# Two ways to carry attention values to the output: merged weights on averaged inputs, or token-wise values averaged head by head

## The chip, the cores and the metric

The kernel runs on one core of a Trainium2 chip. The metric is device time in microseconds (us), the median of several executions; lower is better. The profile is one execution taken with the hardware profiler. Its engines are TensorE (PE, with the weight loads as a row of their own, PEld), VectorE (DVE), ScalarE (ACT), GpSimd (POOL), and the queues that issue transfers (SP, and ACT's and POOL's own).

## What is computed

The input is 2048 tokens of 128 features. It goes through a transformer of six layers, a selective state-space block, and the same transformer once more, with residual sums around them. The change touches the transformer alone. One layer of it, cut to what matters here:

```python
x = normalised input
qkv = shift_tokens(x) @ Wqkv            # 16 heads of 64 features each for q, k and v
q, k = rotary(l2norm(q) * qs), rotary(l2norm(k) * ks)
# windows of 32 tokens: each looks at its own window and at the one before it
attn = softmax(mask(q . k * 8))         # 32 x 64 per head and window
x = x + concat_heads(attn @ v) @ Wo     # Wo: 1024 x 128
a, gate = split(layernorm(shift_tokens(x)) @ W1 + b1)
x = x + (a * gelu(gate)) @ W2 + b2
```

## The kernel before, in words

Activations are kept with the 128 features on the partitions and the 2048 tokens along the free axis (`r0` before attention, `r1` after it). A layer is cut into 16 tiles of 128 tokens (four windows), and the feed-forward part works on blocks of 512 tokens, four tiles each. Everything is float32, and TensorE runs each float32 matmul as two records (x2 in its counts), except transposes, which are one.

`run` goes through 96 + 7 iterations, and in each of them through the list `ORDER`. An entry `("PX", 4)` means: the step PX for the tile whose number is 4 less than that of the iteration. Steps of different tiles thus stand beside each other, and the order in the list is the order in which each of PE, DVE, ACT and POOL runs its own instructions (`manual_schedule`); SP is not in that set. Feed-forward steps (F1, XC, SF, V, VE, XN, G, GL, A, H, Y, YR) run only for every fourth tile.

The steps of one tile, with lines of the profile:

- PQ, PK (`project`, L263): queries and keys, two matmuls each, 128x128 weights against 512 columns, into a double PSUM bank.
- SQ, SK (L275), UQ, UK (L302): squares on ACT and their sums per head on DVE. NL (`roots`, L311 to L316): ACT clips the sums, takes a logarithm and an exponential for a first inverse root, and squares it. NN (`norms`, L320 and L322): one Newton step in two small DVE instructions. T1, T2 (L281, L287), A (L296), C (L326): the rotary products on DVE, their sum and the scaling by the norm on POOL.
- RQ, RK (`turn`, L339): eight transposes each; EQ, EK (L348, L353): copies out of PSUM; EP (L360): the last 32 keys of the tile before.
- S (`score`, L376 and L387): the mask, then 64 matmuls of 64x32 weights against 64 columns, packed into eight sub-arrays of TensorE (two halves of the rows by four quarters of the columns).
- ES, MX, SB, EX, SM, DV: softmax with ACT, DVE and POOL; TP (`flip`, L435): DVE transposes the probabilities in 32x32 squares.
- XT, EXW (`inputs`, `inputs_out`, L442 to L454): the tile's input is transposed to tokens on the partitions and copied out, and two transfers on ACT's queue (48 KB and 16 KB) make a copy that is shifted by one window.
- PX (`average`, L465): the *inputs*, not the values, are averaged by the probabilities: eight matmuls with 32x128 weights and 512 columns (16 heads by 32 queries), four of them side by side in the four quarters of the rows. EZ0, EZ1 (L477): two copies of 128x1024 out of PSUM.
- ZM (`mix`, L485): 16 matmuls, one per head, with 128x128 weights against 128 columns, add up over the heads. The weights are `m`, the product of a head's value weights and output weights. `merge` (L207, L214) makes them once per layer in the first pass and stores them in memory; the second pass loads them.
- RS (L495): residual sum on DVE.
- VE (`variance_out`, L534 to L537) makes the feed-forward norm's variance and first inverse root on ACT; XN (`normal`, L544 to L548) is its Newton step and product, five instructions of 128x512 on POOL.

PSUM has a ring of three double banks (tag `w`: x_ps, t_ps, s_ps, z_ps, two thirds of g_ps and a_ps) and one of two single banks (tag `n`: i_ps, y_ps, c_ps, v_ps, o_ps and the rest). A step that takes a bank waits until the readers of the tile that had it are done.

Of the kernel before, what the change touches and what calls it, by code (L numbers as in the profile page):

```python
# [61 lines left out]
    ("SB", 3), ("GL", 7), ("PK", 0), ("AQ", 1), ("T1K", 0), ("SK", 0), ("ZM", 5), ("UQ", 1),  # L62
    ("RS", 5), ("T2K", 0), ("A", 7), ("EX", 3), ("XN", 6), ("RK", 2), ("H", 7), ("RQ", 2),
    ("EK", 2), ("SM", 3), ("UK", 0), ("EQ", 2), ("NL", 1), ("F1", 5), ("XT", 3), ("NN", 1),
    ("PX", 4), ("PQ", 0), ("AK", 0), ("EP", 2), ("DV", 3), ("EZ0", 4), ("CQ", 1), ("CK", 1),
    ("XC", 5), ("S", 2), ("EXW", 3), ("SF", 5), ("EZ1", 4), ("T2Q", 0), ("V", 5), ("ES", 2),
    ("TB", 3), ("T1Q", 0), ("G", 6), ("Y", 7), ("SQ", 0), ("MX", 2), ("VE", 5), ("TP", 3),
    ("YR", 7),
# [76 lines left out]
class Transformer:  # L145
# [7 lines left out]
    def __init__(self, k, x, again, sb, wp, ps):  # L153
        self.k, self.nc, self.x, self.again = k, k.nc, x, again
        self.sb, self.wp, self.ps = sb, wp, ps
        self.at = [Ctx() for _ in range(DEPTH * NT)]
        for st in self.at:
            st.x, st.rot, st.sq, st.t2 = {}, {}, {}, {}
        self.ff = [Ctx() for _ in range(DEPTH * NB)]
        self.w = [Ctx() for _ in range(DEPTH)]  # L160
        self.tabs = {}
        self.r0 = wp.tile([P, PAD + N + 1], F32, tag="r0", name="r0", bufs=1)
        self.r1 = wp.tile([P, PAD + N + 1], F32, tag="r1", name="r1", bufs=1)
# [9 lines left out]
    def load(self, layer):  # L173
        nc, k, wp, w = self.nc, self.k, self.wp, self.w[layer]
        w.qk = wp.tile([P, 2 * INNER], F32, tag="qk", name="qk")
        nc.sync.dma_start(out=w.qk, in_=k.d_wqk[layer])
        if self.again:
            w.m = wp.tile([P, 8, 2, P], F32, tag="m", name="m")
            nc.sync.dma_start(out=w.m.rearrange("p c j f -> p (c j f)"), in_=k.merged[layer])
            return  # L180
        w.v = wp.tile([P, 8, P], F32, tag="wv", name="wv", bufs=1)
        nc.sync.dma_start(out=w.v, in_=k.d_wv[layer].rearrange("(c p) f -> p c f", p=P))
        w.o = wp.tile([P, 8, P], F32, tag="wo", name="wo", bufs=1)
# [11 lines left out]

    def merge(self, layer):

        nc, w = self.nc, self.w[layer]
        if self.again:
            return  # L200
        w.m = self.wp.tile([P, 8, 2, P], F32, tag="m", name="m")
        for half in range(2):
            m_ps = self.bank2("m_ps").rearrange("p j (c f) -> p j c f", f=P)
            for c in range(4):
                for par in range(2):
                    rows = slice(64 * par, 64 * par + 64)
                    nc.tensor.matmul(  # L207
                        out=m_ps[:, par, c, :],
                        lhsT=w.v[rows, 4 * half + c, :],
                        rhs=w.o[rows, 4 * half + c, :],  # L210
                        start=True,
                        stop=True,
                    )
            nc.scalar.copy(  # L214
                w.m[:, 4 * half : 4 * half + 4].rearrange("p c j f -> p j c f"), m_ps
            )
        nc.sync.dma_start(
            out=self.k.merged[layer], in_=w.m.rearrange("p c j f -> p (c j f)")
        )

    def biases(self, layer):
# [19 lines left out]
        nc.scalar.activation(w.w1, w.w1, AF.Identity, scale=self.vec(V_G + layer))  # L241
# [17 lines left out]
    def project(self, g, kind):  # L259
        nc, st = self.nc, self.at[g]  # L260
        x = self.bank2("x_ps")
        for j in range(2):
# [3 lines left out]
                rhs=self.w[g // NT].qk[:, bass.ds(kind * INNER + j * 512, 512)],  # L266
# [3 lines left out]
        st.x[kind] = x.rearrange("p j (h d) -> p (j h) d", d=DH)  # L270
# [36 lines left out]


    def roots(self, g):
        nc, k, st = self.nc, self.k, self.at[g]  # L310
        nc.scalar.activation(st.ss, st.ss, AF.Relu, bias=k.minus_tiny)  # L311
        st.y = self.sb.tile([P, 2, HEADS], F32, tag="y0", name="y0")
        nc.scalar.activation(st.y, st.ss, AF.Ln, bias=k.tiny)
# [4 lines left out]
    def norms(self, g):  # L318
        nc, st = self.nc, self.at[g]
        nc.vector.scalar_tensor_tensor(st.y2, st.ss, 1e-24, st.y2, ALU.add, ALU.mult)  # L320
        st.rn = self.sb.tile([P, 2, HEADS], F32, tag="rn", name="rn")
        nc.vector.scalar_tensor_tensor(st.rn, st.y2, 1.5, st.y, ALU.subtract, ALU.mult)  # L322
# [116 lines left out]
    def inputs(self, g):  # L439
        st = self.at[g]  # L440
        st.i_ps = self.bank("i_ps")[:, 0:P]
        self.nc.tensor.transpose(  # L442
            st.i_ps, self.r0[:, bass.ds(PAD + g % NT * P, P)], self.k.ident
        )

    def inputs_out(self, g):


        nc, st = self.nc, self.at[g]
        st.xw = self.sb.tile([P, 2, P], F32, tag="xw", name="xw", bufs=3)  # L450
        nc.scalar.copy(st.xw[:, 1], st.i_ps)
        nc.scalar.dma_start(out=st.xw[WIN:, 0], in_=st.xw[0 : P - WIN, 1])
        if g % NT:
            nc.scalar.dma_start(out=st.xw[0:WIN, 0], in_=self.at[g - 1].xw[P - WIN :, 1])  # L454
        else:
            nc.gpsimd.memset(st.xw[0:WIN, 0], 0.0)

    def average(self, g):

        st = self.at[g]  # L460
        st.z = [self.bank2("z_ps"), self.bank2("z_ps")]
        for j in range(2):
            for b in range(4):
                rows = slice(32 * b, 32 * b + 32)
                self.nc.tensor.matmul(  # L465
                    out=st.z[b // 2][:, b % 2].rearrange("p (h q) -> p h q", q=WIN),
                    lhsT=st.xw[rows, j, :],
                    rhs=st.pt[rows, :, j, :],
                    start=(j == 0),
                    stop=(j == 1),  # L470
                )

    def averages_out(self, g, half):
        st = self.at[g]
        if half == 0:
            st.zt = self.sb.tile([P, 4, HEADS, WIN], F32, tag="zt", name="zt")
        self.nc.scalar.copy(  # L477
            st.zt[:, 2 * half : 2 * half + 2].rearrange("p b h q -> p b (h q)"), st.z[half]
        )

    def mix(self, g):
        st = self.at[g]
        st.y_ps = self.bank("y_ps")[:, 0:P]
        for h in range(HEADS):
            self.nc.tensor.matmul(  # L485
                out=st.y_ps.rearrange("p (b q) -> p b q", q=WIN),
                lhsT=self.w[g // NT].m[:, h // 2, h % 2, :],
                rhs=st.zt[:, :, h, :],
                start=(h == 0),
                stop=(h == HEADS - 1),  # L490
# [40 lines left out]
    def variance_out(self, f):  # L531
        nc, k, sb, ff = self.nc, self.k, self.sb, self.ff[f]
        ff.ve = sb.tile([P, 512], F32, tag="ve2", name="ve", bufs=1)
        nc.scalar.activation(ff.ve, ff.v_ps, AF.Identity, bias=k.eps, scale=1.0 / P)  # L534
        ff.rs = sb.tile([P, 512], F32, tag="fsq", name="rs", bufs=1)
        nc.scalar.activation(ff.rs, ff.ve, AF.Ln)
        nc.scalar.activation(ff.rs, ff.rs, AF.Exp, scale=-0.5)  # L537

    def normal(self, f):


        nc, ff = self.nc, self.ff[f]
        ff.xn = t = self.sb.tile([P, 512], F32, tag="xn", name="xn", bufs=1)
        nc.gpsimd.tensor_tensor(t, ff.rs, ff.rs, ALU.mult)  # L544
        nc.gpsimd.tensor_tensor(t, t, ff.ve, ALU.mult)
        nc.gpsimd.tensor_scalar(t, t, -0.5, 1.5, ALU.mult, ALU.add)
        nc.gpsimd.tensor_tensor(t, t, ff.rs, ALU.mult)
        nc.gpsimd.tensor_tensor(t, ff.xc, t, ALU.mult)  # L548
# [523 lines left out]
```

## Time and profile before

| what | us |
|---|---|
| median of 3 runs (lowest, highest) | 3694.47 (3687.63, 3701.53) |
| the profiled execution | 3694.83 |
| its span, first to last instruction | 3693.0 |
| first pass: first q/k projection, last matmul of the last layer (L263, L600) | 43.3, 1608.7 |
| second pass: the same | 2105.8, 3681.0 |

Between the passes lies the state-space block. 1.8 us of the profiled execution lie outside its span.

A row of the table of groups gives line, engine, operation, what is written and read with shapes, and the count; then busy time in us and the mean of one in ns; then the idle time of the engine just before such instructions and what ended it. Busy times of PE overlap and their ends are modelled: how long a step holds TensorE is read from the start of its first matmul to the start of the next step's first, in the timeline. In a table of stretches, each engine's busy time is followed by the count of its instructions in brackets.

### The profile page before, as it was taken

The numbers are of one execution on the slowest core, as the hardware profiler recorded it, in microseconds if no ns is written. First come the engines' busy times: TensorE is split into PE (matmuls) and PEld (weight loads), VectorE is DVE, ScalarE is ACT, GpSimd is POOL, SyncE is SP. The second block draws the span as 40 slices with busy tenths as digits, with TensorE's granted clock in tenths as the row PEclk, the third lists the DMA queues.
The fourth block names the chain that finished last, engine by engine and source line by source line (L and its number), as shares of the span: only waits on it lengthen the run. The fifth ranks groups of instructions, "written<-read, shape, count | busy, mean of one in ns | idle before, by whom it ended". The sixth has DMA issues, their size and how long they took to land.

```text
span 3693.0 us, 93340 instructions
## 1 busy us (share of the span) xinstructions
PE 3483.3 (94%) x41200; PEld 2167.3 (59%) x41200; DVE 3020.2 (82%) x3477; ACT 2338.7 (63%) x3414; POOL 2784.8 (75%) x1606
## 2 busy tenths in 40 slices
PE   6999999999999999976999879999999999999997
PEld 3666666666666666632222345666666666666664
DVE  4988888888888888737988767888888888888883
ACT  3767676767767676734222267767676767676764
POOL 5989989898889898720100188999899998998983
PEclk8999999999999999986877889999999999999998
DMA  3010010100100000000000100010100000000000
GB/s 110 12 52 12 23 46 17 40 23 23 35 29 17 29 12 12 6 7 0 0 0 0 68 10 17 22 34 12 35 23 29 23 22 24 28 18 11 17 6 15
DMA packets 64893, 85.12 MB, mean 23 GB/s; under 512 B 8364, under 2 KB 53352, under 8 KB 61416
## 3 DMA queue, kind: packets, MB, share of 16 engines
q1 hardware_dynamic: 34344, 66.74, 5.4%
q10 hardware_dynamic: 30144, 12.41, 1.5%
q8 instruction: 324, 5.31, 0.6%
q14 instruction: 81, 0.66, 0.1%
HBM read 59.39 MB, written 7.34 MB: 18 GB/s over the span
## 4 chain that ended last, share of the span: by engine, by line
PE 78%; DVE 10%; issue 5%; ACT 4%; POOL 2%; ACTq 1%; DMA 0%; POOLq 0%; SPq 0%; DVEq 0%
PE x_ps L263 18%; PE y_ps L485 17%; PE z_ps L465 10%; PE s_ps L387 7%; PE t_ps L339 4%; PE g_ps L556 4%; PE a_ps L556 3%; PE o_ps L600 3%; DVE t L287 3%; PE y L863 3%; DVE st L856 2%; PE s_ps L376 2%; PE c_ps L845 1%; DVE r L495 1%; PE b_ps L845 1%
## 5 line engine op out<-in xcount | busy, mean ns | idle before, releaser
L296 POOL TENSOR_TENSOR rot<-rot,t 128x1024 f32<-128x1024 f32 x384 | 907.3, 2368 | 209.7 <-DVE t L287 207.6
L485 PEld LDWEIGHTS y_ps<-zt,m 128*128 128x128 f32 x6144 | 720.5, 193 | 99.0 <-issue 88.5
L263 PE MATMUL x_ps<-qk,r 128*128 128x512 f32 x1536 | 758.6, 617 | 10.3 <-ACT sq L275 5.1
L326 POOL TENSOR_TENSOR rot<-rot,rn 128x1024 f32<-128x1024 f32 x384 | 722.4, 1902 | 49.6 <-DVE rn L322 49.4
L485 PE MATMUL y_ps<-zt,m 128*128 128x128 f32 x6144 | 722.8, 276 | 5.9 <-ACT zt L477 5.5
L275 ACT ACTIVATE sq<-x_ps 128x1024 f32<-128x1024 f32 x384 | 394.7, 1028 | 378.8 <-DVE rot L281 378.0
L287 DVE TENSOR_TENSOR t<-x_ps,tab 128x1024 f32<-128x1024 f32 x384 | 469.3, 1222 | 82.9 <-PE x_ps L263 73.9
L263 PEld LDWEIGHTS x_ps<-qk,r 128*128 128x128 f32 x1536 | 271.7, 192 | 421.4 <-issue 226.4
L477 ACT COPY zt<-z_ps 128x1024 f32<-128x1024 f32 x384 | 384.9, 1003 | 205.8 <-PE x_ps L263 157.9
L281 DVE TENSOR_TENSOR rot<-x_ps,tab 128x1024 f32<-128x1024 f32 x384 | 464.1, 1209 | 23.4 <-PE x_ps L263 22.0
L302 DVE TENSOR_REDUCE ss<-sq 128x16 f32<-128x1024 f32 x384 | 454.3, 1183 | 0.1
L409 POOL TENSOR_TENSOR pr<-pr,mx 128x1024 f32<-128x1024 f32 x192 | 365.0, 1901 | 76.1 <-DVE mx L403 76.1
L465 PE MATMUL z_ps<-pt,xw 32*128 32x512 f32 x3072 | 400.8, 614 | 13.1 <-DVE t L287 5.2
L339 PE MATMUL t_ps<-cs,rot 128*128 128x128 f32 x3072 | 370.1, 274 | 19.7 <-POOL rot L326 19.7
L425 POOL TENSOR_TENSOR pr<-pr,rs 128x1024 f32<-128x1024 f32 x192 | 365.2, 1902 | 21.3 <-DVE rs L421 13.4
L339 PEld LDWEIGHTS t_ps<-cs,rot 128*128 128x128 f32 x3072 | 345.8, 142 | 50.1 <-issue 25.6
L403 DVE TENSOR_REDUCE mx<-s_ps 128x16 f32<-128x1024 f32 x192 | 235.0, 1224 | 127.1 <-ACT pr L398 125.4
L387 PE MATMUL s_ps<-kt,qt 64*32 64x64 f32 x24576 | 298.5, 227 | 7.0 <-ACT kt L360 7.0
L387 PEld LDWEIGHTS s_ps<-kt,qt 64*32 64x32 f32 x24576 | 267.0, 105 | 55.0 <-issue 45.9
L353 ACT COPY kt<-t_ps 128x1024 f32<-128x1024 f32 x192 | 194.6, 1013 | 146.6 <-PE t_ps L339 143.1
L435 DVE STREAM_TRANSPOSE pt<-pr 128x1024 f32<-128x1024 f32 x192 | 237.4, 1237 | 43.0 <-POOL pr L425 43.0
L850 ACT ACTIVATE da<-delta,a_neg 128x512 f32<-128x512 f32 x128 | 92.2, 722 | 260.3 <-DVE st L856 255.6
(144 smaller groups left out, 4903.2 us busy)
## 6 DMA issues: line engine op xcount, KB each, us to landing
tab<-in_tabs_dram SPq DMA_DIRECT2D x48, 512.0 KB, 3.6
qk<-in_wqk_dram SPq DMA_DIRECT2D x12, 1024.0 KB
m<-m SPq DMA_DIRECT2D x12, 1024.0 KB, 6.4
xw<-xw ACTq DMA_DIRECT2D x192, 48.0 KB, 1.9
w<-in_w_dram SPq DMA_DIRECT2D x12, 341.0 KB, 7.9
wv<-in_wv_dram SPq DMA_DIRECT2D x6, 512.0 KB, 4.3
wo<-in_wo_dram SPq DMA_DIRECT2D x6, 512.0 KB, 8.4
xw<-xw ACTq DMA_DIRECT2D x180, 16.0 KB, 1.9
```

The lines of the kernel that those rows point to most:

```text
L263: nc.tensor.matmul(out=x[:, j], lhsT=self.r0[:, bass.ds(PAD + g % NT * P, P)], rhs=self.w[g // NT].qk[:, bass.ds(kind * INNER + j * 512, 5 ...
L275: self.nc.scalar.activation(st.sq[kind], st.x[kind], AF.Square)
L281: self.nc.vector.tensor_tensor(st.rot[kind], st.x[kind], cos, ALU.mult)
L287: self.nc.vector.tensor_tensor(st.t2[kind].rearrange("p h (two c) -> p h two c", two=2), st.x[kind].rearrange("p h (two c) -> p h two c", ...
L296: self.nc.gpsimd.tensor_tensor(st.rot[kind], st.rot[kind], st.t2[kind], ALU.add)
L302: self.nc.vector.tensor_reduce(st.ss[:, kind, :], st.sq[kind], AX.X, ALU.add)
L326: self.nc.gpsimd.tensor_tensor(st.rot[kind], st.rot[kind], st.rn[:, kind, :].unsqueeze(2).to_broadcast([P, HEADS, DH]), ALU.mult,)
L339: self.nc.tensor.transpose(t_ps[:, c, :], flat[:, bass.ts(c, P)], self.k.ident)
L387: nc.tensor.matmul(out=st.s[32 * b : 32 * b + 32, par, c, :], lhsT=st.qt[rows, c, bass.ts(b, WIN)], rhs=st.kt[rows, c, bass.ds(WIN * b, 2 ...
L465: self.nc.tensor.matmul(out=st.z[b // 2][:, b % 2].rearrange("p (h q) -> p h q", q=WIN), lhsT=st.xw[rows, j, :], rhs=st.pt[rows, :, j, :], ...
L477: self.nc.scalar.copy(st.zt[:, 2 * half : 2 * half + 2].rearrange("p b h q -> p b (h q)"), st.z[half])
L485: self.nc.tensor.matmul(out=st.y_ps.rearrange("p (b q) -> p b q", q=WIN), lhsT=self.w[g // NT].m[:, h // 2, h % 2, :], rhs=st.zt[:, :, h, ...
```

## The change

- Layers load all of Wqkv (`w.qkv`) and Wo (`w.o`). `merge` and the stored product are gone.
- XT and EXW are gone. PV projects the values of a tile (two matmuls as in PQ) into another double bank of the ring, EV copies them out on ACT (128x1024), and VD issues two transfers on SP that make the copy shifted by one window (96 and 32 partitions by 4 KB, that is 384 KB and 128 KB).
- PX works head by head: for each head, window and key window, a matmul with 32x64 weights (values) against 32 columns (probabilities), 128 in all, into eight sub-arrays (four quarters of the rows by two halves of the columns). Its output is half as large, so EZ0 and EZ1 copy 128x512 each.
- ZM uses the output weights: eight matmuls of 128x128 weights against 128 columns.
- NL loses its clipping instruction; a new step FL clips on POOL. NN is three small POOL instructions in place of two on DVE.
- The feed-forward norm stays in PSUM: VE is three ACT instructions, VT does the Newton step in two DVE instructions of 128x512 that read and, the first of them, write `v_ps`. Their result has its sign turned, which `minus_g` in the weights undoes. XN keeps one POOL product.
- `ORDER` is another list, with other lags.

```diff
 ORDER = (
-    ("SB", 3), ("GL", 7), ("PK", 0), ("AQ", 1), ("T1K", 0), ("SK", 0), ("ZM", 5), ("UQ", 1),
-    ("RS", 5), ("T2K", 0), ("A", 7), ("EX", 3), ("XN", 6), ("RK", 2), ("H", 7), ("RQ", 2),
-    ("EK", 2), ("SM", 3), ("UK", 0), ("EQ", 2), ("NL", 1), ("F1", 5), ("XT", 3), ("NN", 1),
-    ("PX", 4), ("PQ", 0), ("AK", 0), ("EP", 2), ("DV", 3), ("EZ0", 4), ("CQ", 1), ("CK", 1),
-    ("XC", 5), ("S", 2), ("EXW", 3), ("SF", 5), ("EZ1", 4), ("T2Q", 0), ("V", 5), ("ES", 2),
-    ("TB", 3), ("T1Q", 0), ("G", 6), ("Y", 7), ("SQ", 0), ("MX", 2), ("VE", 5), ("TP", 3),
-    ("YR", 7),
+    ("VT", 6), ("VD", 3), ("EQ", 2), ("AK", 1), ("UK", 1), ("F1", 5), ("EX", 3), ("S", 2),
+    ("EZ0", 4), ("XC", 5), ("SF", 5), ("EZ1", 4), ("PK", 0), ("UQ", 1), ("FL", 1), ("TB", 7),
+    ("SM", 3), ("V", 5), ("XN", 6), ("ES", 2), ("Y", 7), ("PQ", 0), ("MX", 2), ("NL", 1),
+    ("SK", 0), ("T2K", 0), ("DV", 3), ("G", 6), ("NN", 1), ("CK", 1), ("CQ", 1), ("SB", 2),
+    ("T1K", 0), ("PV", 2), ("SQ", 0), ("YR", 7), ("VE", 5), ("T2Q", 0), ("T1Q", 0), ("A", 6),
+    ("TP", 3), ("GL", 6), ("EV", 2), ("RK", 1), ("H", 6), ("EK", 1), ("AQ", 0), ("ZM", 4),
+    ("EP", 1), ("RQ", 1), ("RS", 4), ("PX", 3),
 )
...
-        if self.again:
-            w.m = wp.tile([P, 8, 2, P], F32, tag="m", name="m")
-            nc.sync.dma_start(out=w.m.rearrange("p c j f -> p (c j f)"), in_=k.merged[layer])
-            return
...
+        w.qkv = wp.tile([P, 3 * INNER], F32, tag="qkv", name="qkv")
+        nc.sync.dma_start(out=w.qkv, in_=k.d_wqkv[layer])
+        w.o = wp.tile([P, 8, P], F32, tag="wo", name="wo")
...
-    def merge(self, layer):
...
-        nc.scalar.activation(w.w1, w.w1, AF.Identity, scale=self.vec(V_G + layer))
+        nc.scalar.activation(w.w1, w.w1, AF.Identity, scale=k.minus_g[:, layer : layer + 1])
...
+        if kind == 2:
+            st.v_ps = x
...
+    def floors(self, g):
+        ss = self.at[g].ss
+        self.nc.gpsimd.tensor_scalar(ss, ss, 1e-24, None, ALU.max)
...
-        nc.scalar.activation(st.ss, st.ss, AF.Relu, bias=k.minus_tiny)
...
-        nc.vector.scalar_tensor_tensor(st.y2, st.ss, 1e-24, st.y2, ALU.add, ALU.mult)
         st.rn = self.sb.tile([P, 2, HEADS], F32, tag="rn", name="rn")
-        nc.vector.scalar_tensor_tensor(st.rn, st.y2, 1.5, st.y, ALU.subtract, ALU.mult)
+        nc.gpsimd.tensor_tensor(st.rn, st.ss, st.y2, ALU.mult)
+        nc.gpsimd.tensor_scalar(st.rn, st.rn, -1.0, 1.5, ALU.mult, ALU.add)
+        nc.gpsimd.tensor_tensor(st.rn, st.rn, st.y, ALU.mult)
...
-    def inputs(self, g):
-    def inputs_out(self, g):
...
+    def values_out(self, g):
         nc, st = self.nc, self.at[g]
+        st.v = self.sb.tile([P, HEADS, DH], F32, tag="v", name="v")
+        nc.scalar.copy(st.v.rearrange("p h d -> p (h d)"), st.v_ps.rearrange("p j f -> p (j f)"))
+
+    def values_before(self, g):
+        nc, st = self.nc, self.at[g]
+        st.vb = self.sb.tile([P, HEADS, DH], F32, tag="vb", name="vb")
+        nc.sync.dma_start(out=st.vb[WIN:], in_=st.v[0 : P - WIN])
         if g % NT:
+            nc.sync.dma_start(out=st.vb[0:WIN], in_=self.at[g - 1].v[P - WIN :])
         else:
+            nc.gpsimd.memset(st.vb[0:WIN], 0.0)
...
         st.z = [self.bank2("z_ps"), self.bank2("z_ps")]
+        for c in range(8):
+            for j, v in enumerate((st.vb, st.v)):
+                for b in range(4):
+                    rows = slice(32 * b, 32 * b + 32)
+                    for par in range(2):
+                        self.nc.tensor.matmul(
+                            out=st.z[b // 2][64 * par : 64 * par + 64, b % 2, bass.ts(c, WIN)],
+                            lhsT=v[rows, 2 * c + par, :],
+                            rhs=st.pt[rows, 2 * c + par, j, :],
+                            start=(j == 0),
+                            stop=(j == 1),
+                        )
...
+            st.zt = self.sb.tile([P, 8, 4, WIN], F32, tag="zt", name="zt")
         self.nc.scalar.copy(
+            st.zt[:, :, 2 * half : 2 * half + 2].rearrange("p c b q -> p b c q"),
+            st.z[half][:, :, 0:256].rearrange("p b (c q) -> p b c q", q=WIN),
         )
...
+        for c in range(8):
             self.nc.tensor.matmul(
+                out=st.y_ps,
+                lhsT=self.w[g // NT].o[:, c, :],
+                rhs=st.zt[:, c].rearrange("p b q -> p (b q)"),
+                start=(c == 0),
+                stop=(c == 7),
             )
...
+    def deviation(self, f):
+
         nc, k, sb, ff = self.nc, self.k, self.sb, self.ff[f]
...
+        nc.scalar.activation(ff.rs, ff.v_ps, AF.Ln, bias=k.eps, scale=1.0 / P)
         nc.scalar.activation(ff.rs, ff.rs, AF.Exp, scale=-0.5)
+        ff.xn = sb.tile([P, 512], F32, tag="xn", name="xn", bufs=1)
+        nc.scalar.activation(ff.xn, ff.rs, AF.Square, scale=float(np.sqrt(0.5 / P)))
+
+    def newton(self, f):
+
+        nc, ff = self.nc, self.ff[f]
+        nc.vector.scalar_tensor_tensor(ff.v_ps, ff.v_ps, P * LN_EPS, ff.xn, ALU.add, ALU.mult)
+        nc.vector.scalar_tensor_tensor(ff.xn, ff.v_ps, 1.5, ff.rs, ALU.subtract, ALU.mult)
 
     def normal(self, f):
 
+        ff = self.ff[f]
+        self.nc.gpsimd.tensor_tensor(ff.xn, ff.xc, ff.xn, ALU.mult)
...
```

## The prediction

> **What bounds the kernel now.** I read the page first (busy shares, then the chain that ended last), then the table of stretches, then TensorE's timeline. The page and, below it, the stretch of 16 iterations in the middle of the first pass:
>
> ```profile
> PE 3483.3 (94%) x41200; PEld 2167.3 (59%) x41200; DVE 3020.2 (82%) x3477; ACT 2338.7 (63%) x3414; POOL 2784.8 (75%) x1606
> ...
> PE 78%; DVE 10%; issue 5%; ACT 4%; POOL 2%; ACTq 1%; DMA 0%; POOLq 0%; SPq 0%; DVEq 0%
> ```
>
> ```profile
> core 0: us, PE busy (x) PEld busy (x) DVE busy (x) ACT busy (x) POOL busy (x), PEclk, DMA share, GB/s
> 726.88:980.10 253.22, 251.07 (x3385) 166.70 (x3383) 219.70 (x247) 180.83 (x266) 226.22 (x123) 1.00 0.10 29
> ```
>
> TensorE is busy 251.07 of 253.22 us at the full granted clock. One tile takes 253.22/16 = 15.83 us, in which POOL works 14.14, DVE 13.73 and ACT 11.30 us. So inside the two passes (192 tiles) only TensorE's own steps count, until another engine passes them. What each step holds is read from start to start in TensorE's timeline; the first stretch is one iteration without feed-forward matmuls but with Y (o_ps), the last two lines are from another:
>
> ```profile
> 880.55 2.18 PE L465 MATMUL z_ps<-pt,xw 32*128 32x512 f32 x16
> 882.66 1.98 PE L263 MATMUL x_ps<-qk,r 128*128 128x512 f32 x4
> 884.58 0.39 PE L376 MATMUL s_ps<-masks 32*128 32x512 bf16 x2
> 884.90 1.56 PE L387 MATMUL s_ps<-kt,qt 64*32 64x64 f32 x128
> 886.39 2.85 PE L600 MATMUL o_ps<-h,w 128*128 128x512 f32 x6
> 889.07 1.88 PE L263 MATMUL x_ps<-qk,r 128*128 128x512 f32 x4
> 890.79 3.73 PE L485 MATMUL y_ps<-zt,m 128*128 128x128 f32 x32
> 894.36 1.91 PE L339 MATMUL t_ps<-cs,rot 128*128 128x128 f32 x16
> 896.11 0.27 PE L442 MATMUL i_ps<-cs,r 128*128 128x128 f32 x1
> 896.46 2.02 PE L465 MATMUL z_ps<-pt,xw 32*128 32x512 f32 x16
> 898.41 1.98 PE L263 MATMUL x_ps<-qk,r 128*128 128x512 f32 x4
> ...
> 711.43 1.16 PE L207 MATMUL m_ps<-wo,wv 64*128 64x128 f32 x16
> ...
> 714.51 1.99 PE L263 MATMUL x_ps<-qk,r 128*128 128x512 f32 x4
> ```
>
> **TensorE's steps, one by one.**
>
> *PV added:* the same four records as PQ, 882.66 to 884.58: **+1.92** us a tile.
>
> *ZM halved:* 32 records take 890.79 to 894.36 = 3.57; 16 of them 1.79: **-1.79**.
>
> *XT gone:* 896.11 to 896.46 = 0.35, but part of it is the gap ahead of the packed step, which stays. At least one transpose (1.75/16 = 0.11) goes, at most 0.35. I take **-0.20**.
>
> *merge gone:* 711.43 to 714.51 = 3.08 for each of five layers inside the first pass: **-15** us in all. The sixth lies among the waits of the start and is taken as nothing.
>
> *PX:* now 1.95 and 2.11, say 2.03. It becomes 128 matmuls, 256 records, of 32x64 weights and 32 columns. The trace has none of that shape; the nearest is the score, 128 records that also run in eight sub-arrays, with 64x32 weights and 64 columns. It takes 884.90 to 886.39 = 1.49, elsewhere 613.38 to 615.06 = 1.68. That burst, cut in three:
>
> ```profile
> 613.37:613.64 0.27, 0.26 (x32) 0.27 (x33) 1.00 0.00 0
> 613.64:614.72 1.08, 1.08 (x124) 1.08 (x100) 1.00 0.27 61
> 614.72:615.06 0.34, 0.21 (x17) 0.04 (x4) 1.00 0.18 48
> ```
>
> (Stretch and length, TensorE's busy time with records in it, weight loads likewise.) The first 32 records, which had stood ready, start within 0.27 us, 8.4 ns each; the other 96 (124 less 28 still running) within 1.08, 11.25 ns each; then 0.15 to 0.34 passes until the next step starts. Is the slower pace set by the columns streamed or by the count of loads and matmuls? The new step streams as many columns in all (128 x 32 against 64 x 64) and has twice the records, each load twice as wide. Lower bound, by columns: 1.49. Upper, by loads: a 128-column load with its matmul takes 3.57/32 = 112 ns in ZM; half of it, an estimate, is 56 ns for 64 columns; four at once (PX's 16 records of 512 columns take 122 ns each, against 480 in PQ, so four quarters do run together) make 14 ns, 256 x 14 = 3.6, with the tail 3.9. I take the pace of the nearest row, since halving the columns while doubling the load should about cancel within one sub-array: 0.27 + 224 x 11.25 ns + 0.2 = 3.0, **+0.97**.
>
> Sum per tile: 1.92 - 1.79 - 0.20 + 0.97 = +0.90; 192 x 0.90 = +173; less 15: **+158 us**.
>
> [...]
>
> **Edits costed at nothing, and their cover.** A tile has 16.7 us of TensorE after the change.
>
> *ACT:* the two zt copies shrink from 1.00 each to about 0.59 (the 128x512 copy at L518), EV adds 1.01 (as L353), the 0.27 copy and the 0.33 clipping go: -0.4, and the two issues on its queue (0.52 and 0.61) go as well. 10.9 of 16.7.
>
> *DVE:* L320 and L322 go (0.55 and 1.00), VT adds two of about 0.74 (L587, which also reads PSUM) per four tiles: -1.18, 12.6 of 16.7. TensorE didn't wait for these, so nothing is won.
>
> *POOL:* XN loses 1.04 + 1.27 + 0.62 + 1.27 per four tiles, -1.05 a tile. Four instructions of 128x32 come in. Lower bound: 1024 elements take 2.37 us and 512 take 1.27, so 0.17 is left at no elements. Upper: 1.04, the 128x4 power at L108. I take 0.33, the 128x1 copy at L860: +1.3, so 14.4 of 16.7. At the upper bound POOL has 17.3 and is the bound, 0.6 x 192 = 115 us more.
>
> *VD:* its transfers wait for EV in the iteration before; PX, the last entry of its own iteration, needs them. The 512 KB table lands 3.6 us after its issue; there is most of an iteration, some 16 us. Behind VD on SP stand the table and weight loads; the table product on POOL, every fourth iteration, now stands early and may wait for some of those 3.6 us, which POOL's 2.3 spare us a tile cover.
>
> *The ring of three double banks* is taken eight times a tile, not seven. RK takes PK's bank, RQ takes PQ's, and PX needs TP. From PK's end the readers run SK 1.03, T2K 1.22, T1K 1.21, T2Q 1.22, T1Q 1.21, TP 1.24 = 7.13 us and handovers of some 0.05 to 0.1 each, 7.5. TensorE meanwhile has PQ, PV, RK, ZM, RQ: 1.92 + 1.92 + 0.87 + 1.79 + 0.87 = 7.37. That is level. In the iterations without feed-forward work (one in four) a wait of 0.1 to 0.3 us ahead of PX may appear, 5 to 15 us in all; I leave it to the range.
>
> The profiled execution took 3694.83, its span 3693.0; the median of the runs is 0.4 lower. 3694.8 + 158 = **3852 us**.
>
> **Rivals.**
>
> *Not slower: PX goes by its columns.* Decides if its pace over the whole burst stays under 7.9 ns a record (PX under 2.18 us, where the sum is zero). For it: the columns are equal, and ready records start 8.4 ns apart. Against: after 32 records the pace fell to 11.25. By columns alone PX takes 1.5 and the kernel 3694.8 + 192 x (-0.07 - 0.53) - 15 = 3565; at 2.0 it is 3660. Faster by over 0.5%, about what a measurement of this kernel can tell from no change: 0.12. Between 3676 and 3713 (a pace near 8.3 ns): 0.08.
>
> *PX goes by its loads:* 3.9 us, so 192 x (1.87 - 0.07) - 15 = +331, 4026 us. If loads for the two column halves also wait for one another and only two run at once, 28 ns each, 7.2 us and some 4660. Against: the score's first 32 loads start as fast as its matmuls. 0.13 for the first, 0.03 for the second.
>
> *A new wait takes over:* the chain through DVE above, or POOL with slow small instructions. One microsecond in each iteration without feed-forward work adds 48, giving 3900; POOL at its upper bound 3967. 0.10.
>
> **How the numbers follow.** My forecast, PX between 2.6 and 3.5 us, has the remaining 0.54 and spans 3775 to 3948. The range runs from 3670, which takes in a PX of 2.05, to 4050, past the load-bound case; outside lie most of the faster rival (about 0.11) and the worst of the loads and waits (about 0.07). Slower by over 0.5%: 0.54 + 0.16 + 0.10 = 0.80.
>
> **What would show it.** In TensorE's timeline, z_ps with x256 from its first start to the next step's: 3.0 right, under 2.2 or over 3.6 a rival. x_ps three times in an iteration, y_ps with x16 at 1.79. TensorE still 98% busy in the passes; if it falls under 96%, the waits name the reader (T1K or TP on DVE, or POOL's scaling). POOL's 128x32 rows near 0.33. I am wrong altogether if TensorE stops being the bound.

## The result and the profile after

| what | before, us | after, us |
|---|---|---|
| median of 4 runs each (lowest, highest) | 3692.37 (3687.63, 3701.53) | 4925.79 (4905.74, 4941.46) |
| the profiled execution | 3694.83 | 4913.81 |
| its span | 3693.0 | 4912.0 |
| mean granted TensorE clock | 0.952 | 0.815 |

The changed kernel is slower: ratio 1.3334, 95% interval 1.3269 to 1.3398. The forecast of 3852 us had the sign and missed the size nearly eightfold: +1219 us between the two profiled executions where +158 was worked out. The page of the changed kernel, with the same rows as before:

```profile
PE 4077.7 (83%) x84592; PEld 2552.7 (52%) x84592; DVE 2806.0 (57%) x3188; ACT 2275.9 (46%) x3210; POOL 2786.7 (57%) x2182
...
PEclk7888888787888888887898888888888788887887
...
q8 instruction: 664, 10.88, 0.9%
...
PE 72%; issue 17%; DVE 6%; ACT 2%; POOL 2%; DMA 0%; POOLq 0%; DVEq 0%; SPq 0%; ACTq 0%
```

No other engine took over: DVE and POOL fell to 57%. TensorE itself stands idle for 17% of the chain, put down to "issue": nothing that the profile shows held it. The clock row reads 8, where before it read 9 nearly throughout. And there is a queue that the prediction never looked at: q8 brings *instructions*. 10.88 MB in 664 packets are 16 KB a packet. The trace has 84592 loads, 84592 matmuls and 829 instructions of the sequencer for TensorE; at 256 to a packet these 170013 make 664.1 packets. Before, 82895 make 323.8, and the page has 324. So a packet is a block of 256 instructions of TensorE, or 128 pairs of a load and a matmul. The change took the loads and matmuls of a tile from 429 to 881.

The table of stretches, 300 us inside the first pass:

```profile
core 0: us, PE busy (x) PEld busy (x) DVE busy (x) ACT busy (x) POOL busy (x), PEclk, DMA share, GB/s
1000.00:1300.00 300.00, 255.37 (x5695) 166.35 (x5694) 169.17 (x188) 148.10 (x210) 193.07 (x144) 0.81 0.14 39
```

TensorE works 85% of the stretch, where it was 99% (251.07 of 253.22). The waits of TensorE (total, times, longest) name the two packed steps, PX (z_ps) and S (s_ps):

```profile
PE z_ps L437 <- issue: 502.9, 233, 5.9
PE s_ps L361 <- issue: 149.1, 142, 2.1
```

One iteration in TensorE's timeline, from within PX on; further rows of PX, each of a few records, are left out:

```profile
1010.72 0.34 PE L437 MATMUL z_ps<-pt,v 32*64 32x32 f32 x6 [2.31 <-issue]
...
1012.02 0.49 PE L437 MATMUL z_ps<-pt,v 32*64 32x32 f32 x13
1012.44 0.61 PE L350 MATMUL s_ps<-masks 32*128 32x512 bf16 x2
1012.98 0.63 PE L361 MATMUL s_ps<-kt,qt 64*32 64x64 f32 x19
1014.47 1.81 PE L361 MATMUL s_ps<-kt,qt 64*32 64x64 f32 x109 [0.86 <-issue]
1016.20 5.68 PE L232 MATMUL x_ps<-qkv,r 128*128 128x512 f32 x8
1021.72 2.74 PE L530 MATMUL g_ps<-xn,w 128*128 128x512 f32 x6
...
1028.59 1.04 PE L313 MATMUL t_ps<-cs,rot 128*128 128x128 f32 x8
1029.46 1.95 PE L458 MATMUL y_ps<-zt,wo 128*128 128x128 f32 x16
1031.25 1.04 PE L313 MATMUL t_ps<-cs,rot 128*128 128x128 f32 x8
```

PX stands still for 2.31 us in the middle of its own records, S once more for 0.86 after 19 records. The eight records of projections that follow take 5.52 us (1016.20 to 1021.72), 690 ns each, where four took 1.92 before: over 4.02 us of this stretch the granted clock is 0.5. ZM (L458) takes its 1.79 as forecast (1029.46 to 1031.25). The instruction packets of the trace fit the stop: one starts at 1008.33, the last record before the stop is at 1008.20, the next at 1010.72, 2.4 us after the packet's start. And the stops come at the edges of blocks: of 178 pairs of successive stops inside one burst (a row of small matmuls without other work between them), 177 are 128 or 256 records, that is one or two blocks, apart.

Where the 1219 us came from, summed over all records of the trace from the start of one to the start of the next:

| tile (step) | before | after | difference | predicted |
|---|---|---|---|---|
| z_ps (PX) | 401 | 1144 | +743 | +186 |
| x_ps (PQ, PK, now PV) | 767 | 1318 | +551 | +369 |
| s_ps (masks, S) | 379 | 677 | +298 | 0 |
| y_ps (ZM) | 694 | 351 | -343 | -344 |
| i_ps, m_ps (XT, merge) | 83 | 0 | -83 | -53 |
| t_ps, c_ps, all others | | | +51 | 0 |

The differences, before rounding, add up to the 1219 us.

### The profile page after: what moved, and what is told of

Read it like the earlier page. It is cut to its first block, busy times and chain, and to the rows that moved or that the text cites. A ratio compares the mean times of both kernels' runs of the same rounds, so it can differ in the third digit from the quotient of the medians.

```text
span 4912.0 us, 181224 instructions
## 1 busy us (share of the span) xinstructions
PE 4077.7 (83%) x84592; PEld 2552.7 (52%) x84592; DVE 2806.0 (57%) x3188; ACT 2275.9 (46%) x3210; POOL 2786.7 (57%) x2182
## 3 DMA queue, kind: packets, MB, share of 16 engines
q1 hardware_dynamic: 62760, 159.56, 11.2%
q8 instruction: 664, 10.88, 0.9%
## 4 chain that ended last, share of the span: by engine, by line
PE 72%; issue 17%; DVE 6%; ACT 2%; POOL 2%; DMA 0%; POOLq 0%; DVEq 0%; SPq 0%; ACTq 0%
PE x_ps L232 22%; PE z_ps L437 13%; PE s_ps L361 8%; PE y_ps L458 7%; PE t_ps L313 7%; PE o_ps L574 3%; PE g_ps L530 3%; PE a_ps L530 3%; DVE st L828 2%; PE s_ps L350 2%; PE c_ps L480 2%; DVE rot L253 1%; DVE t L259 1%; PE v_ps L502 1%; ACT sq L247 1%
## 5 line engine op out<-in xcount | busy, mean ns | idle before, releaser
L232 PE MATMUL x_ps<-qkv,r 128*128 128x512 f32 x2304 | 1306.2, 715 | 5.3 <-issue 2.9
L232 PEld LDWEIGHTS x_ps<-qkv,r 128*128 128x128 f32 x2304 | 514.3, 233 | 630.4 <-issue 600.2
L437 PE MATMUL z_ps<-pt,v 32*64 32x32 f32 x24576 | 593.6, 240 | 261.4 <-issue 261.2
L437 PE MATMUL z_ps<-pt,vb 32*64 32x32 f32 x24576 | 575.7, 238 | 244.9 <-issue 241.8
L437 PEld LDWEIGHTS z_ps<-pt,vb 32*64 32x64 f32 x24576 | 524.6, 143 | 284.8 <-issue 273.5
L437 PEld LDWEIGHTS z_ps<-pt,v 32*64 32x64 f32 x24576 | 519.4, 147 | 280.4 <-issue 280.1
L361 PE MATMUL s_ps<-kt,qt 64*32 64x64 f32 x24576 | 434.9, 303 | 151.7 <-issue 149.1
L449 ACT COPY zt<-z_ps 128x512 f32<-128x512 f32 x384 | 210.7, 586 | 698.1 <-PE z_ps L437 698.1
L313 PE MATMUL t_ps<-cs,rot 128*128 128x128 f32 x3072 | 407.2, 277 | 42.4 <-POOL rot L300 26.1
L372 ACT COPY pr<-s_ps 128x1024 f32<-128x1024 f32 x192 | 194.4, 1012 | 453.3 <-PE s_ps L361 453.3
L458 PE MATMUL y_ps<-zt,wo 128*128 128x128 f32 x3072 | 378.0, 277 | 2.0 <-ACT zt L449 2.0
```

Source lines behind the costliest of these rows:

```text
L232: nc.tensor.matmul(out=x[:, j], lhsT=self.r0[:, bass.ds(PAD + g % NT * P, P)], rhs=self.w[g // NT].qkv[:, bass.ds(kind * INNER + j * 512, ...
L313: self.nc.tensor.transpose(t_ps[:, c, :], flat[:, bass.ts(c, P)], self.k.ident)
L361: nc.tensor.matmul(out=st.s[32 * b : 32 * b + 32, par, c, :], lhsT=st.qt[rows, c, bass.ts(b, WIN)], rhs=st.kt[rows, c, bass.ds(WIN * b, 2 ...
L437: self.nc.tensor.matmul(out=st.z[b // 2][64 * par : 64 * par + 64, b % 2, bass.ts(c, WIN)], lhsT=v[rows, 2 * c + par, :], rhs=st.pt[rows, ...
L458: self.nc.tensor.matmul(out=st.y_ps, lhsT=self.w[g // NT].o[:, c, :], rhs=st.zt[:, c].rearrange("p b q -> p (b q)"), start=(c == 0), stop= ...
```

## The experiments

**Theory A, formed from the traces after the result:** TensorE's instructions come in blocks of 256, no two closer together than some 3.3 us (3.28 at the least in this trace), and few stand ready when a burst starts; PX and S side by side are 768 instructions in a row, so the burst runs out of instructions, and the stops bring the clock down. **Rival B:** the shifting transfers (512 KB a tile) crowd out the instruction packets. **Rival C:** such small matmuls have a price of their own, by their columns or their loads. **Rival D:** the new order, with its ring of three banks, waits. Where a count of stops is given, it is of gaps over 0.6 us, from start to start, between two records of PX or of S; time at half clock is read from the trace's record of the granted clock (0.5). The changed kernel has 370 stops, 745 us in all, and 1815 us at half clock; the kernel before has none that ends in "issue", and 358 us. A time given without an interval is that of a single run.

### The transfers left out

```diff
-    ("VT", 6), ("VD", 3), ("EQ", 2), ...
+    ("VT", 6), ("EQ", 2), ...
-            for j, v in enumerate((st.vb, st.v)):
+            for j, v in enumerate((st.v, st.v)):
```

> The changed kernel without the step VD: PX reads the unshifted values for both key windows, so no transfer between partitions is made (the output is not the reference's). Instruction counts on TensorE are as in the changed kernel. Theory A, instruction supply (TensorE's instructions come in 16 KB blocks of 256, no two fetches start closer than 3.3 us, and the packed steps PX and S eat a block in 1.2 to 1.5 us): the stops inside z_ps and s_ps stay, 4850 to 4950 us. Rival B, the 512 KB of VD per tile hold up the instruction fetches on the DMA engines: the stops go, under 4200 us.

Measured: 4887.68 us, before 3701.43 beside it; 364 stops, 707 us, 1808 us at half clock. That is 38 us below the changed kernel's median, so the transfers have next to no part in the 1219 us. Rival B falls, and VD is covered, as the prediction had it.

### Half of PX

```diff
-            for j, v in enumerate((st.vb, st.v)):
+            for j, v in ((1, st.v),):
-                            start=(j == 0),
+                            start=True,
```

> The changed kernel with half of PX: only a tile's own key window is averaged, the window before is left out (128 records instead of 256; the output is not the reference's). Theory A: PX and S together ask for 512 instructions and not 768, about one stop of 2 to 3.4 us a tile goes, and with it part of the time at half clock: 4000 to 4350 us. Rival C, the small matmuls are slow at their own pace (9.7 ns a record in the trace of the changed kernel): 128 x 9.7 ns = 1.24 us a tile, 240 us in all, about 4680 us.

Measured: 4070.89 us. PX's median falls from 5.35 to 1.42 us, less than a third for half the matmuls, and the kernel loses 843 us. Stops: 201, 402 us; half clock 815 us; 472 packets. The waits of TensorE:

```profile
PE s_ps L361 <- issue: 253.8, 165, 3.5
PE z_ps L437 <- issue: 103.7, 42, 4.0
```

Of PX's 230 stops (555 us) 40 are left (112 us), while S, which stands right behind it and is unchanged, now has 161 (290 us) where it had 140 (190 us). A price of PX's own matmuls can't move stops into S; a supply that PX uses up can.

### S moved away from PX

```diff
-    ("VT", 6), ("VD", 3), ("EQ", 2), ("AK", 1), ("UK", 1), ("F1", 5), ("EX", 3), ("S", 2),
+    ("VT", 6), ("VD", 3), ("EQ", 2), ("AK", 1), ("UK", 1), ("F1", 5), ("EX", 3),
...
-    ("SM", 3), ("V", 5), ("XN", 6), ("ES", 2), ("Y", 7), ("PQ", 0), ("MX", 2), ("NL", 1),
-    ("SK", 0), ("T2K", 0), ("DV", 3), ("G", 6), ("NN", 1), ("CK", 1), ("CQ", 1), ("SB", 2),
-    ("T1K", 0), ("PV", 2), ...
+    ("SM", 3), ("V", 5), ("XN", 6), ("Y", 7), ("PQ", 0), ("NL", 1), ("S", 2),
+    ("SK", 0), ("T2K", 0), ("DV", 3), ("T1K", 0), ("ES", 2), ("MX", 2), ("G", 6), ("NN", 1),
+    ("CK", 1), ("CQ", 1), ("SB", 2), ("PV", 2), ...
```

> The changed kernel with one change of order: S no longer follows PX, it stands behind PK and PQ (its readers ES and MX, and SK, T2K, T1K, are moved to fit); all work is done. Theory A: PK and PQ, 3.8 us with few instructions, let one more block arrive between the two packed bursts: one stop of 2 to 3.4 us a tile less, 4250 to 4550 us. Rival C: the order of the bursts changes nothing in their own pace, 4850 to 4950 us. Rival D, the ring of three double banks: the new order makes PV wait for T1K, and it gets slower, over 4950 us.

Measured: 4783.29 us, outside A's range. Its timeline:

```profile
1001.06 0.27 PE L438 MATMUL z_ps<-pt,v 32*64 32x32 f32 x6 [2.05 <-issue]
1001.67 3.28 PE L233 MATMUL x_ps<-qkv,r 128*128 128x512 f32 x4
...
1009.90 1.48 PE L362 MATMUL s_ps<-kt,qt 64*32 64x64 f32 x128
```

S runs its 128 records without a stop in all but two tiles, and its mean is back at 1.60 us (2.98 in the changed kernel, 1.60 before): 264 us gained. PX still stops (mean 5.58), and the four records of a projection, now right behind it, take 3.28 us (1.92 before). All projections together cost 136 us more than in the changed kernel, and the transposes 55 more. Counted from start to start, a wait stands with the step ahead of it: the transposes behind PV wait for the bank that the score's readers hold, and PX behind the last transposes for a bank that ACT copies out:

```profile
PE z_ps L438 <- issue: 455.0, 217, 4.9
PE t_ps L314 <- DVE mx L378: 68.9, 137, 0.5
PE z_ps L438 <- ACT qt L323: 51.8, 44, 1.2
```

So A is right for S, and D's waits give part of it back. Moving a burst is worth what its new neighbours leave of it.

### The score twice, in the kernel before

```diff
-        for c in range(8):
+        for n, c in enumerate([*range(8), *range(8)]):
...
-                        stop=(c == 7),
+                        stop=(n == 15),
```

> The kernel before, with the 64 matmuls of S issued twice (the scores come out doubled; the output is not the reference's): 256 records in one burst of a shape whose pace is known, and nothing else of the change. By pace alone 128 more at 11.25 ns are 1.44 us a tile: 3692 + 276 = about 3970 us. Theory A: a burst of 512 instructions runs past what is stored, with a stop of 1 to 2.4 us in most tiles and time at half clock behind it: 4150 to 4600 us.

Measured: 4371.33 us. The old kernel, which had no stop in S, now has 182 (390 us) and 481 us at half clock. S takes 4.81 us, three times its 1.60 for twice the records. Its waits, then a burst in its timeline:

```profile
PE s_ps L387 <- issue: 351.0, 183, 4.7
```

```profile
889.53 2.31 PE L387 MATMUL s_ps<-kt,qt 64*32 64x64 f32 x206
893.67 0.74 PE L387 MATMUL s_ps<-kt,qt 64*32 64x64 f32 x50 [1.83 <-issue]
894.34 1.12 PE L529 MATMUL v_ps<-sq,ones 128*128 128x512 f32 x2
```

206 records at 11.2 ns, then nothing for 1.83 us, then the rest. None of the change's edits is in this kernel: a burst of 256 pairs is enough. In 182 of its 192 bursts there is one stop, after 135 to 255 pairs: none at the first edge of a block in the burst, nearly always one at the second.

### Two heads in one matmul

All the work of the change, with half of PX's instructions: the weights are the values of two heads (32x128), the moving side the probabilities of both (64 columns). Half of what comes out (each head by the other's probabilities) is not copied.

```diff
-                    for par in range(2):
-                        self.nc.tensor.matmul(
-                            out=st.z[b // 2][64 * par : 64 * par + 64, b % 2, bass.ts(c, WIN)],
-                            lhsT=v[rows, 2 * c + par, :],
-                            rhs=st.pt[rows, 2 * c + par, j, :],
+                    self.nc.tensor.matmul(
+                        out=st.z[b // 2][:, b % 2, bass.ts(c, 64)],
+                        lhsT=v[rows, 2 * c : 2 * c + 2, :].rearrange("p h d -> p (h d)"),
+                        rhs=st.pt[rows, 2 * c : 2 * c + 2, j, :],
...
-        self.nc.scalar.copy(
-            st.zt[:, :, 2 * half : 2 * half + 2].rearrange("p c b q -> p b c q"),
+        for par in range(2):
+            rows = slice(64 * par, 64 * par + 64)
+            self.nc.scalar.copy(
+                st.zt[rows, :, 2 * half : 2 * half + 2].rearrange("p c b q -> p b c q"),
```

> The changed kernel, PX with two heads at a time: 64 matmuls of 32x128 weights against 64 columns (half of each result is not used; the copies out of PSUM become four of 64 partitions). All work is done, the columns streamed by all matmuls of PX are as many as in the changed kernel, the instructions half. Theory A, instruction supply: 512 instructions in PX and S together, and a block in PX lasts longer because the 128-column loads bound it (107 ns each, four at once, 27 ns a record, 3.4 us): most stops go and the clock stays up, 3950 to 4200 us. Rival C, own pace of small matmuls (9.7 ns a record or by columns): 4650 to 4900 us.

Measured: 4081.82 us (four runs), ratio to before 1.109, interval 1.1034 to 1.1146. 625 loads and matmuls a tile, 64 stops (79 us; 42 of them in S), 416 us at half clock, mean clock 0.949. Its waits:

```profile
PE s_ps L361 <- issue: 45.1, 54, 2.2
...
PE z_ps L436 <- issue: 23.0, 27, 2.3
```

844 us of the change's 1233 (medians) go with half of one step's instructions; the columns and loads per instruction became *wider*. PX's median is 3.62 us, 28 ns a record where the expectation has 27 from loads of 107 ns; in the trace of the kernel before, loads of 128 columns start 108 to 109 ns apart where they follow closest (x_ps, t_ps). With 3.62 in place of 3.0 the prediction's own sum gives 3694.8 + 192 x (3.62 - 2.03 - 0.07) - 15 = 3972; the 110 us left lie in PX's own stops and half clock (its mean is 3.94, 61 us), in S (1.82 in place of 1.60, 42 us) and in the transposes (35 us), less some 30 that XT and the merge saved beyond the forecast.

The same with the order of the third experiment, to take away the last stops:

> As e6_two_heads, with S behind PK and PQ as in e3_score_later: no burst of over 256 instructions is left. Theory A: no stops inside z_ps and s_ps at all, the clock at 0.93 or more over the span; what remains is the sum of TensorE's steps with PX at 3.4 to 3.6 us, 3970 to 4000, and the waits for the ring that e3 showed, up to 180 us: 3950 to 4150 us. Rival C: 4550 to 4800 us.

Measured: 4275.57 us, worse, and outside the expectation. 13 stops are left (18 us), 2 of them in S, but the ring of banks took their place:

```profile
DVE t L260 <- ACT sq L248: 838.2, 182, 9.5
```

```profile
PE x_ps L233 <- DVE rot L254: 105.8, 89, 4.0
```

DVE waits 838 us for ACT's squares (158 without the move), and TensorE then for DVE's rotary products, the readers of its banks. This order is no cure where the stops are few.

### Twice the columns, as many instructions

```diff
-                            out=st.z[b // 2][64 * par : 64 * par + 64, b % 2, bass.ts(c, WIN)],
+                            out=st.z[b // 2][64 * par : 64 * par + 64, b % 2, bass.ts(c, 64)],
-                            rhs=st.pt[rows, 2 * c + par, j, :],
+                            rhs=st.pt[rows, 2 * c : 2 * c + 2, j, :],
```

(with the copies of the two-head kernel)

> The changed kernel with 64 columns in every matmul of PX in place of 32 (the other head's probabilities are streamed too and their results not used; copies out of PSUM as in e6): as many instructions as in the changed kernel, twice the columns. Theory A: the burst is bound by the supply of instructions, so the wider matmuls cost next to nothing: 4800 to 5050 us. Rival C by columns: PX's 256 records at 9.7 ns become twice as long, 2.5 us a tile, 5300 to 5450 us.

Measured: 4865.51 us, 371 stops, 709 us. PX's mean is 5.82 us, against 5.90 with half the columns. Its row in the table of groups:

```profile
L437 PE MATMUL z_ps<-pt,v 32*64 32x64 f32 x24576 | 616.4, 241 | 245.4 <-issue 245.4
```

and that of the changed kernel:

```profile
L437 PE MATMUL z_ps<-pt,v 32*64 32x32 f32 x24576 | 593.6, 240 | 261.4 <-issue 261.2
```

A record lasts 241 ns at 64 columns and 240 at 32, and the idle time before them hardly differs. With supply, the first 128 records of a burst start every 10.6 ns at 64 columns and every 9.7 at 32; over 256 records the difference is 0.23 us, and it vanishes in the waiting for instructions. Rival C falls: by the columns here, by the loads with the 9.7 ns, as the loads start no slower (in the changed kernel 127 in 1.222 us after the first, 9.6 ns each). Leaving the transfers out gave 38 us and doubling the columns cost nothing (60 us below the changed kernel's median); half of PX's instructions (two heads in one) gave 844.

### The norms in the kernel before

The prediction put the edits on the norms at nothing. They were put into the old kernel: all of them (first), the feed-forward norm alone (second), and all with NN six entries later (third).

```diff
-    ("SB", 3), ("GL", 7), ...
+    ("VT", 6), ("SB", 3), ("GL", 7), ...
-    ... ("EQ", 2), ("NL", 1), ("F1", 5), ("XT", 3), ("NN", 1),
+    ... ("EQ", 2), ("FL", 1), ("NL", 1), ("F1", 5), ("XT", 3), ("NN", 1),
```

(and FL, NL, NN, VE, VT, XN as in the change)

> The kernel before with the norms' part of the change alone (FL and NN on POOL, VT in PSUM on DVE, one POOL product in XN, the sign in the weights), in the order of before with FL ahead of NL and VT at the head of the list. Prediction on record: nothing is won or lost by these edits, 3680 to 3705 us. Rival: POOL's small instructions delay the scaling and with it the transposes, over 3730 us.

Measured: 3812.01 us, ratio 1.036, interval 1.0304 to 1.0416. Not nothing. In the table of groups of this kernel, the row of POOL's first Newton instruction:

```profile
L324 POOL TENSOR_TENSOR rn<-ss,y 128x32 f32<-128x32 f32 x192 | 48.4, 252 | 424.9 <-ACT y L319 422.4 <-ACT kt L364 2.6
```

An instruction of 0.25 us stands 2.2 us a tile (422.4 / 192) in POOL's queue until ACT's roots arrive, and holds back the rotary sums and scalings behind it.

> The kernel before with the feed-forward norm's part alone (VT on DVE in PSUM, one POOL product in XN, the sign in the weights; VT at the head of the order). If this part is what made e5_norms_alone slower, about 3810 us. If it was NN on POOL, this one is 3670 to 3700 us: TensorE is the bound and POOL and DVE have room.

Measured: 3761.71 us, ratio 1.0184, interval 1.0132 to 1.0237, between the two expectations. Half of the 3.6% is there without the attention norm's edits, and it is VT's: it stands on DVE ahead of T2K, waits for the ACT steps of the feed-forward norm, and in every fourth iteration TensorE waits for T2K's bank:

```profile
883.54 0.27 PE L442 MATMUL i_ps<-cs,r 128*128 128x128 f32 x1
885.61 2.01 PE L465 MATMUL z_ps<-pt,xw 32*128 32x512 f32 x16 [1.80 <-DVE t L287]
```

> e5_norms_alone with NN moved behind DV, right ahead of CQ, so that POOL runs AK and DV while ACT makes the roots. If e5's loss is POOL standing still between FL and NN (1.0 us a tile and 4 us of other POOL work behind it): back to 3680 to 3710 us. If it is the work itself (three instructions more on POOL, 0.25 us each): still about 3800 us.

Measured: 3741.00 us, ratio 1.014, interval 1.0099 to 1.0181, again between the two expectations: NN's half is gone with six places in the list, VT's stays.

Then VT was moved, in the kernel with the feed-forward norm alone:

```diff
-    ("VT", 6), ("SB", 3), ("GL", 7), ...
-    ("RS", 5), ("T2K", 0), ("A", 7), ("EX", 3), ("XN", 6), ...
+    ("SB", 3), ("GL", 7), ...
+    ("RS", 5), ("T2K", 0), ("A", 7), ("EX", 3), ("VT", 6), ("XN", 6), ...
```

> e9_vt_alone with VT moved from the head of the order to the place right ahead of XN, behind T1K, UQ, RS and T2K on DVE. If e9's loss is VT standing ahead of T2K, whose PSUM bank PX waits for (1.8 us in every fourth iteration, 86 us in all): 3660 to 3700 us, no slower than before, and perhaps a little faster, as POOL loses four instructions. If the loss is the work of VT itself or the longer hold of v_ps: about 3750 us.

Measured: 3737.90 us, ratio 1.0176, interval 1.0134 to 1.0217. That fits the second branch (about 3750), not the first: the wait went to another place and kept its size (i_ps in the kernel with VT ahead takes 77 us more than before, here g_ps takes 74 more).

```profile
888.97 2.81 PE L557 MATMUL g_ps<-xn,w 128*128 128x512 f32 x6
893.36 1.98 PE L263 MATMUL x_ps<-qk,r 128*128 128x512 f32 x4 [1.58 <-ACT sq L275]
```

In both places DVE's two added instructions (0.70 and 0.69 us) come before a reader of the ring that TensorE waits for; `v_ps`, which VT holds longer, is in neither wait. At 87% of an iteration (13.73 of 15.83) DVE was not the bound, and still had no slack at these points.

Last, the attention norm as it was (clip on ACT, Newton on DVE, no FL), but in the two-head kernel with the new order:

```diff
-    ("UQ", 1), ("FL", 1), ("TB", 7),
+    ("UQ", 1), ("TB", 7),
-        nc.gpsimd.tensor_tensor(st.rn, st.ss, st.y2, ALU.mult)
-        nc.gpsimd.tensor_scalar(st.rn, st.rn, -1.0, 1.5, ALU.mult, ALU.add)
-        nc.gpsimd.tensor_tensor(st.rn, st.rn, st.y, ALU.mult)
+        nc.vector.scalar_tensor_tensor(st.y2, st.ss, 1e-24, st.y2, ALU.add, ALU.mult)
+        nc.vector.scalar_tensor_tensor(st.rn, st.y2, 1.5, st.y, ALU.subtract, ALU.mult)
```

> e6_two_heads with the attention norms as before (clipping on ACT, Newton step on DVE, no FL). If POOL's wait for the roots costs in the changed order too: 3950 to 4040 us. If there POOL has the room: 4060 to 4120 us, no gain over e6's 4082.

Measured: 4195.89 us, ratio to before 1.1379 (1.1334 to 1.1424), 114 us *worse* than with the Newton step on POOL; neither expectation holds. POOL now waits for DVE's `rn`, and TensorE's transposes for POOL:

```profile
POOL rot L296 <- DVE rn L292: 940.3, 192, 10.5
```

```profile
PEld t_ps L309 <- POOL rot L296: 313.9, 141, 11.8
```

So the same edit costs about 70 us in one order (3812 to 3741 by taking its wait away) and saves 114 in another. No kernel of these beats the one before.

## Why the prediction was wrong

**The step that failed** is the price of PX: "I take the pace of the nearest row", with the sum 0.27 + 224 x 11.25 ns + 0.2 = 3.0 us. The pace was right, even cautious: while it has instructions, PX starts 127 records in 1.234 us after the first, 9.7 ns each. What failed was to stretch the pace of a burst of 128 records over 384 in a row (PX and, right behind it, S). The score is 256 instructions: one block. PX and S are three, and the smallest spacing of two blocks in any run here lies between 3.23 and 3.42 us, where TensorE can use a block up in 128 x 9.7 ns = 1.2 us. So PX took 5.9 us in the mean in place of 3.0, and S, which the sum put at no change, went from 1.60 to 2.98.

The bound could have been read from the kernel before. Its page has the line `q8 instruction: 324, 5.31, 0.6%`, and of the 323 spacings of these packets in its trace 25 are under 4 us, the smallest 3.25. Three blocks at 3.4 us are 10.2 us, less what stands ready when the burst starts; PX, the masks and S took 9.2. How much stands ready is the author's estimate from the doubled score: no stop at the first edge of a block and one at the second (after 135 to 255 pairs) fit the rest of one block and the whole of the next. No run varied it.

**The second thing missing is the clock.** The prediction had it at full speed throughout. In the changed kernel the granted clock falls to 0.5 214 times, for stretches of 3.4, 6.8 or 10.2 us (5th, 50th and 95th percentile), 1815 us in all; 192 of the falls come within 6.83 us of the start of a stop. A projection's record takes 429 ns from start to start at the full clock and 853 at half; 591 of them fell into half clock (24 before). 591 x 0.424 = 250 us covers the whole excess of x_ps over its predicted +369 (182). A record of S takes 10.4 ns at the full clock, 14.2 at half: about 85 us of its 264, the rest is waiting for instructions. Stops and clock go together over the runs: 370 stops and 1815 us at half clock, 217 and 1331, 201 and 815, 182 and 481, 64 and 416, none and 358. With few stops the two part (13 stops, 471 us at half clock): there TensorE also waits for the ring. In the 3.41 us before a fall, as long as the shortest of these stretches, the longest pause was 1.8 us in the median over the 214 falls. That the stops bring the clock down was not shown by itself: no run had the stops without the lower clock, so their shares are read from the records, not from a run.

**The rivals.** None of them had instruction supply in it. "PX goes by its loads" named the nearest times (4026, and 4660 with 7.2 us for PX if the column halves wait for one another), for another reason: with supply PX starts a record every 9.7 ns, under the 14 and 28 ns of its two cases. Its way of reckoning, a whole load with its matmul (112 ns) shared by four quarters, 28 ns, is what the 128-column loads of the two-head PX show (128 records in 3.62 us). "If it falls under 96%, the waits name the reader": TensorE fell to 85%, and the waits named no reader but "issue". "I am wrong altogether if TensorE stops being the bound" did not foresee that it could be the bound without working.

**What was right:** a projection's four records at full clock (1.80 where 1.92 was taken for PV), ZM at 1.79, XT (0.32 a tile, inside the 0.11 to 0.35), the shift's cover (taken away, under 1%), zt's copies (0.586 against "about 0.59"), POOL's small instructions (0.22 to 0.29 where 0.33 was taken). The merge gave 22 us where 15 were taken. The doubt whether two column halves load side by side went the right way too: nothing in PX's pace (9.7 ns a record) shows them waiting for one another.

**The edits costed at nothing** are covered in the changed kernel: inside the two passes TensorE's largest wait there for another engine is for POOL's scaling, 26.1 us in all (19.7 before), and none of its waits names VT. POOL stands 949 us for ACT's roots there, and TensorE loses no more than that 26.1 us behind it. Whether the edits would be covered without TensorE's stops was not tried. In the old order they cost 3.6%: half by a POOL instruction that waits in its queue for ACT, half by 1.4 us of DVE work in every fourth iteration. The working compared sums of busy time with the length of an iteration ("12.6 of 16.7"). Such a sum shows that an engine isn't the bound, not that an instruction's place in its queue is free.

## What to carry to other kernels

Before packing a step into many small matmuls, count the pairs of loads and matmuls that stand in a row, neighbouring steps included, and set them against the instruction packets of the kernel's own trace: here two packets of 128 pairs came no closer than 3.23 to 3.42 us in any run, and PX, while supplied, started as many in 1.23. If it doesn't fit, make each instruction do more (two heads at once won back 844 us though half its result is thrown away) before moving steps, which shifts the waits of everything around. And an edit "hidden" by an engine's average slack is hidden only if its place in that engine's queue has the slack: the same edits on the attention norm cost 70 us in one order and saved 114 in another.

## What the hardware showed unexpectedly

- TensorE's instruction blocks (16 KB, 256 instructions) came no closer than 3.23 to 3.42 us in any run, and after a stop records went on 2.2 to 2.9 us after a block's packet had started (2.4 in the median of the changed kernel's 370 stops). What sets the spacing was not tried.
- While supplied, 32x64 weights with 32 columns in eight sub-arrays start every 9.7 ns, with 64 columns every 10.6; the whole burst took as long with either (5.90 and 5.82 us).
- Loads of 128 columns in the four quarters of the rows run side by side: 128 records in 3.62 us, 28 ns each, where ZM's loads of the whole 128x128 array take 112 ns with their matmul.
- In the 3.41 us ahead of each of the changed kernel's 214 falls to a granted clock of 0.5, the longest pause was 1.8 us in the median. Whether such pauses are enough by themselves was not tried.
